# Cross attention with an adapter: queries and output as fp32r products of halves, y and z by DMA, and a new order

## The chip, the cores and the metric

The kernel runs on one core of a Trainium2 chip. The metric is the device time of one execution in microseconds (us); a lower one is better. Times are medians over runs of the same program. The engines are PE (matrix products), DVE (vector), ACT (scalar functions), POOL (general) and SP, which here only issues the DMAs. PE's results go to banks of 512 columns in PSUM; other operands lie in SBUF.

## The reference

Two batches of 2048 rows of 640 features, eight heads of 80 features. Of 128 context tokens 124 are text, and the last four feed an adapter.

```python
query = hidden_states @ Wq
keyt = enc @ Wk
valt = enc @ Wv
hs = _mha(query, keyt, valt)
ca_q1 = jnp.einsum('btc,th->bch', ca, Wq_ca)
ca_q1 = ca_q1[:, indices, :]
ca_hs1 = _mha(ca_q1, residual, residual)
ca_q2 = ca_hs1 @ Wq
ca_hs2 = _mha(ca_q2, ca_k2, ca_v2)
out = hs + ca_hs2
out = out @ Wout + b_out
out = out + residual
```

`indices` spreads 384 rows of `ca_q1` over the 2048 rows; `residual` is x. All inputs and the output are fp32.

## The kernel before

The rows are cut in eight blocks of 512 (four a batch) and in 16 units of 256, two for each block. The work has two strands.

*The text strand.* A block of x is loaded (`xi`) and transposed on DVE (`xt`). `queries_fast` multiplies it by Wq: 640 features are five chunks of 128; the first four form a 2 x 2 scheme in which seven products of halves, with sums of halves of x (`x_sums`) and of Wq (`wq_sums`), stand for eight, and the fifth chunk is multiplied plainly. Block 0 is multiplied plainly altogether (`pq_first`). DVE or ACT take the results out of the bank, DVE adds the second ones (`q<-q,pq`). Parts of the fifth chunk travel through memory to other partitions (`away`, `landing`, then `rests`). For each tile of 128 rows, text scores `sc` follow, their maxima `m` on DVE, exponentials `p` on ACT, a division on POOL (seldom DVE), a transpose `eb` on DVE, a trip through memory (`kept`, `pT`), and the products `ph` with the values, which give `hs`. `text_out_fast` multiplies `hs` by Wout in products `po` of 320 columns, again seven for eight with sums of `hs` and of Wout, and DVE adds each product to the rows of x that will be stored (`x_more`, `last_rows`).

*The adapter strand.* For each block, `yz_block` makes `yz` on PE (`pyz`), ACT copies it out; its y rows are transposed (`yt`) and go through memory, its z rows are taken out by a shuffle on DVE (`zs`), for batch 1 by way of memory (`zb`), and split in two fp32r parts (`zop`). In `adapter`, each batch has 24 score tiles of 128 x 2048, called s1 (row `s<-zop,cop`), of which DVE takes maxima (`mx`). After the last of them the maxima are gathered (`most`, `turned`), go through memory into the operand `cop`, and 24 score tiles of a second kind, s2 (`s<-cop,zop`), are made with it, put through an exponential on ACT (`ea`) and multiplied with y (`acc`). s1 and s2 share a single room of four banks (`quad`): a score tile can be written only when the one before has been read.

*The order.* Nothing is scheduled at run time. The class `Desk` has a table, `ORDER`: a list of task numbers written out; each entry lets the next step of that task be issued, a letter choosing the engine (a ACT, v DVE, g POOL). Every engine works through its own queue in exactly that order. A `Room` counts buffers: a step that needs one stands in the table behind the step that frees it. The helper `matmul` pins each product in place and cuts an fp32 weight of 128 columns into four strips of 32, unless PE is already in the full shape:

```python
wide = rows > 64 and cols > 64 and self.mode != (P, P)
for c in range(0, cols, 32) if wide else (0,):
```

Lines 211, 226 and 236 of the profile are the helpers that issue PE's products, the other engines' instructions and SP's transfers; the groups are told apart by their tiles.

Of the kernel before, what the change touches and what calls it, by code (L numbers as in the profile page):

```python
# [14 lines left out]
P = 128  # L15
HEADS = 8
T = 4
# [28 lines left out]
class Do:  # L46
# [4 lines left out]
    def __init__(self, engine, fn, after=None, needs=(), frees=(), marks=()):  # L51
        self.engines = (engine,) if isinstance(engine, str) else engine
        self.fn, self.after, self.needs, self.frees, self.marks = fn, after, needs, frees, marks
        self.slots, self.value = [], None
# [12 lines left out]
class Desk:  # L67
# [3 lines left out]
    SIDES = {"a": "ACT", "v": "DVE", "g": "POOL"}  # L71
# [3 lines left out]
        2 2 2 2 2 2 36 0 0 0 4 4 0 0 0 0 0 0 0 0 4 0 0 111a 6 6 6 0 4 6 4 2 2 2 2 2 2 2 4 113a 107 108 109 110 4 6  # L75
        114a 115a 3 6 3a 3 116v 4 6 3a 3 3v 6 3 8 8 7 7 7 2 15 15 15 11 15 15 12 8 7 0 0 118a 8 5 15 15 15 15 10 7
        117a 15 7 8 7 7 7 120a 9 1 119v 8 6 121a 7 7 7 7 122a 7 7 124v 9 123v 125a 126a 8 8 127 8 9 8 36 5 128 8 8 8 5
        9 9 9 129 5 130 15 36 15 15 131 9 9 14 14 9 14 14 14 14 9 14 6 112 136a 133a 135v 134v 14g 137 36 112 11 112
        15 14 15 36 14 12 14g 36 138 138 138 36 138 138 12 12 12 36 144v 145v 12 36 36 11a 9 9 9 139 11 9 9 9 140 143a
        9 146a 12 13 101 17 106 140 140 140 140 141 18 6 140 140 140 140 142 106 132 132 16 17 147g 148g 132 101v 142  # L80
        132 101v 101g 101g 101g 39 152 152 152 152 152 152 151 17 17 36 36 156a 142 142 142 18 18 18 18 18 18 18 18
        132 142 16 151 152 36 36 142 16 16 157a 43 151 152g 149g 152 16 132 16 101v 101 18 16 16g 36 159 159 16 36 158
        36 101g 150g 101g 17 160a 159 159 16 151 161a 16g 155 18 18 18 152 162 36 153 36 18 158 158 18 158 155 17 155
        153 36 20 20 19 163 159 159 163 163 21 21 171 163 142 142 158 172 164 163 163 36 21 21 172 172 172 172 21 43
        154 36 154 175 175 165 159 36 175 175 175 175 19 19 19 159g 166g 167g 159 36 36 170 39 181a 36 170 21 21 21 21
        172 172 172 19 20 19 19 182 177 176 177 182 175 19g 19 177 177 159 173 36 20 183a 170 20 36 168g 182 182 182
        182 172 19 184a 20 178 170 178 182 169g 175g 17 21 21 21 21 21 21 22 19g 177 174 177 185 23 182g 36 36 185 185
        186a 185 185 175 24 24 24 24 24 175 24 174 174 24 24 188 24 174 187 185 36 22 47 22 22 22 192 22 180 194 179
        36 180 192 192 192 192 22 192 22g 182 190 174 182 36 179 180 36 195 192 196 36 47 174 174 174 158 20 23 202 23
        23 24 24 24 197 22 197 198g 192g 199v 36 192 36 24 201g 24 206a 197 197 197 22 200g 197 23 202 23 208 51 207a  # L90
        208 174 189 208 208 208 208 197 197g 22g 36 209 209 36 202 205 209 214a 209 192 132 197 189 158 189 189 189
        197 132 189 202 36 215a 209 205 189 209 36 216 55 36 203 205 209 217 217 24 209g 36 26 26 217 217 217 217 209
        217 27 27 27 27 27 158 209 210 27 212 27 204 36 204 203 218 51 36 36 225 224 219g 220g 222g 221g 217g 36 193
# [89 lines left out]
    def run(self):  # L183
        for entry in self.ORDER.split():
# [7 lines left out]
            for room, i in op.frees:  # L192
                room.give(i)
            for k in op.marks:
                self.event(k).known = True
# [44 lines left out]
def kernel(  # L240
# [788 lines left out]
    def queries(n, after, first=False):  # L1029
# [5 lines left out]
        def room(s):  # L1035
            q_of[n] = q_slot(s[0], f"q_{n}"), s[0]
# [1136 lines left out]
```

## Time and profile before

| | |
|---|---|
| median of 3 runs | 564.87 us (564.87 to 565.77) |
| span of the profiled execution | 562.6 us, from its first to its last instruction |
| PE busy | 554.5 us (99%) |
| DVE busy | 386.4 us (69%) |
| ACT busy | 265.7 us (47%) |
| POOL busy | 198.4 us (35%) |

The span is the profiled execution's time from the first to the last instruction; the median of the runs is 2.3 us above it, and what lies around the span has no row of its own. A row of a group reads: line, engine, operation, output <- inputs, partitions x elements, number; then the busy time in us and the mean of one in ns; then the time that the engine sat idle ahead of them and who ended it. A row of the timeline begins with start and duration in us. A row of the stretches gives start and end, the length, and for each engine its busy time and number of instructions, then the granted clock, the share of the DMA engines and GB/s. Products overlap in PE's pipeline, so the distance between starts, not the duration, is what one costs.

### The profile page before, as it was taken

The page shows a single profiled execution, that of the slowest core. Times are in us where ns is not written, and L with a number is a line of the kernel's source. Part 1 is how long each engine was busy: PE and PEld are TensorE (multiplying, and loading weights), DVE is VectorE, ACT ScalarE, POOL GpSimd, SP SyncE. Part 2 cuts the span into 40 slices and gives each one's busy share as a digit, 9 for nine tenths or more (in the row PEclk, how much of TensorE's full clock was granted, in tenths as well). Part 3 has the DMA queues.
Part 4 walks back from the last instruction along what each step waited for, and adds up shares of the span by engine and source line. Part 5 has one row for each costly group of instructions (what it writes and reads, how often), then busy time and mean ns, then how long its engine had stood idle before and what let it go on. Part 6 is the DMA issues. An engine that isn't in the chain of part 4 may idle for free.

```text
span 562.6 us, 18845 instructions
## 1 busy us (share of the span) xinstructions
PE 554.5 (99%) x8088; PEld 314.4 (56%) x8088; DVE 386.4 (69%) x622; ACT 265.7 (47%) x733; POOL 198.4 (35%) x211
## 2 busy tenths in 40 slices
PE   9999999999999999999999999999999999999997
PEld 8563445456555555555465445455545666666664
DVE  1457999999996564579999998655635655555534
ACT  3122645445338898886525424579878230100100
POOL 7002534434524523013559364512330513321310
PEclk9999999999999999999999999999999999999999
DMA  8994769774877889455568895758853687688603
GB/s 264 240 172 127 154 119 161 165 169 141 162 198 163 179 249 172 140 170 172 170 138 248 217 236 133 241 163 255 252 165 108 181 186 192 150 262 229 203 28 142
DMA packets 151699, 101.48 MB, mean 180 GB/s; under 512 B 86492, under 2 KB 130156, under 8 KB 151616
## 3 DMA queue, kind: packets, MB, share of 16 engines
q1 hardware_dynamic: 150848, 99.88, 69.6%
q8 instruction: 64, 1.05, 0.8%
q0 software_dynamic: 768, 0.40, 0.4%
q14 instruction: 19, 0.16, 0.1%
HBM read 61.34 MB, written 38.90 MB: 178 GB/s over the span
## 4 chain that ended last, share of the span: by engine, by line
PE 91%; DVE 3%; DMA 3%; ACT 1%; SPq 1%; POOL 1%; issue 0%; ACTq 0%; DVEq 0%
PE po L211 26%; PE pq L211 25%; PE acc L211 8%; PE sc L211 7%; PE ph L211 7%; PE s L211 7%; PE pq_first L211 3%; PE pyz L211 3%; DVE mx L226 2%; PE pk L211 1%; PE unread L215 1%; DMA zb<-z 1%; DMA x_more<-in_x_dram 1%; DMA first_rests<-away 1%; SPq L236 1%; PE pt_wq L219 1%
## 5 line engine op out<-in xcount | busy, mean ns | idle before, releaser
L226 DVE TENSOR_REDUCE mx<-s 128x4 f32<-128x2048 f32 x48 | 109.2, 2275 | 2.5 <-PE s L211 2.4
L226 ACT ACTIVATE p<-sc,m 128x124 f32<-128x124 f32 x256 | 89.5, 374 | 32.2 <-DVE m L226 32.2
L226 ACT ACTIVATE ea<-s 128x2048 f32<-128x2048 f32 x48 | 90.4, 1884 | 26.5 <-PE s L211 26.2
L226 POOL TENSOR_TENSOR p<-p,r 128x992 f32<-128x992 f32 x28 | 51.9, 1857 | 132.9 <-DVE r L226 126.1
L211 PE MATMUL po<-wout_sums,hs 128*32 128x320 f32 (+1 forms) x1012 | 77.8, 433 | 0.5 <-DVE x_more L226 0.5
L211 PE MATMUL po<-wout_sb,hs 128*32 128x320 f32 (+2 forms) x972 | 77.1, 429 | 0.0
L226 DVE TENSOR_TENSOR x_more<-x_more,po 128x320 f32<-128x320 f32 x72 | 33.7, 480 | 42.6 <-PE po L211 42.6
L226 ACT ACTIVATION_READ_ACCUMULATOR p<-sc,m 128x1 f32 x256 | 55.4, 217 | 0.0
L211 PE MATMUL pq<-xt,wq_sb 128*32 128x256 f32 x896 | 54.3, 381 | 0.5 <-DVE q L226 0.5
L211 PEld LDWEIGHTS po<-wout_sums,hs 128*32 128x32 f32 (+1 forms) x1012 | 37.5, 110 | 29.7 <-issue 1.6
L211 PEld LDWEIGHTS po<-wout_sb,hs 128*32 128x32 f32 (+1 forms) x972 | 36.7, 111 | 27.4 <-issue 0.9
L211 PE MATMUL acc<-ea,y_sb 128*32 128x384 f32 (+2 forms) x768 | 50.4, 384 | 0.0
L226 DVE TENSOR_REDUCE m<-sc 128x4 f32<-128x496 f32 x64 | 40.8, 663 | 13.6 <-PE sc L211 13.4
L226 POOL TENSOR_TENSOR hs<-hs 128x256 f32<-128x256 f32 x35 | 27.5, 790 | 63.5 <-DVE hs L226 54.7
L211 PE MATMUL ph<-pT,vpad 128*32 128x256 f32 x768 | 46.7, 380 | 0.2 <-ACT p L226 0.2
L226 DVE TENSOR_TENSOR last_rows<-last_rows,po 128x320 f32<-128x320 f32 (+1 forms) x57 | 26.4, 473 | 24.8 <-PE po L211 24.7
L226 DVE STREAM_TRANSPOSE eb<-p 128x1024 f32<-128x1024 f32 x32 | 39.5, 1234 | 5.3 <-POOL p L226 3.3
L211 PEld LDWEIGHTS pq<-xt,wq_sb 128*32 128x32 f32 x896 | 27.5, 110 | 22.9 <-issue 5.5
L226 ACT COPY hs<-ph 128x512 f32<-128x512 f32 (+1 forms) x23 | 12.1, 541 | 58.9 <-PE ph L211 58.6
L211 PE MATMUL pq<-xt,wq 128*32 128x512 f32 x320 | 38.8, 595 | 0.0
L211 PEld LDWEIGHTS sc<-kmain,q 64*128 64x128 f32 x512 | 31.8, 187 | 11.9 <-issue 7.5
L211 PE MATMUL sc<-kmain,q 64*128 64x124 f32 x512 | 37.5, 283 | 0.2
(197 smaller groups left out, 792.3 us busy)
## 6 DMA issues: line engine op xcount, KB each, us to landing
kept<-eb SPq DMA_DIRECT2D x32, 512.0 KB
pT<-kept SPq DMA_DIRECT2D x48, 256.0 KB
landing<-away SPq DMA_DIRECT2D x60, 128.0 KB
xi<-in_x_dram SPq DMA_DIRECT2D x28, 256.0 KB
x_more<-in_x_dram SPq DMA_DIRECT2D x18, 320.0 KB
out_dram<-x_more SPq DMA_DIRECT2D x18, 320.0 KB
last_rows<-in_x_dram SPq DMA_DIRECT2D x14, 320.0 KB
y<-yt SPq DMA_DIRECT2D x16, 256.0 KB
```

The costliest lines, as they stand in the source:

```text
L211: self.pin(self.nc.tensor.matmul(out[strip], lhsT[:, strip], rhs, **kw))
L215: self.pin(self.nc.tensor.matmul(out, zeros, zeros, start=True, stop=True))
L219: self.pin(self.nc.tensor.transpose(out, in_, ident))
L226: return lambda *args, **kw: self.pin(getattr(engine, what)(*args, **kw))
L236: self.pin(self.nc.sync.dma_start(out, in_))
```

## The change

Each operand of the query and output products is split into a top half, rounded to fp32r after a factor of 1 - 2^-13, and the rest, low. With a third operand, mix = top - 2^12 low, the fp32 product is put together from three fp32r products: top by top plus low by low (in one bank, `pq` or `po`), and mix by mix (`pm`), added with the factors 1 + 2^-12 and -2^-12. A chunk of 128 query features thus takes 5 + 5 + 5 products of 512 columns, and half of an output tile 5 + 5 + 5 of 320. The seven-for-eight schemes and their sums go. The parts of x (`top`, `low`, `mix`) are made on ACT, DVE and POOL (`part_of`, `mix_of`), those of `hs` in `hidden_parts`, those of the weights in `weight_part`. Block 0's queries stay plain fp32.

z no longer goes through the shuffle: four DMAs write its rows to memory and four for each half bring them back repeated (`z_rows`), in both batches. The fifth chunk's parts come back straight in fp32r. There are two rooms for queries for three, two sets of `hs` parts for three, and three of x (two, and a third when the setup's rows are free), which now also hold a block's top and low. Wout is loaded and split after the last block's queries. And `ORDER` is another table altogether; two of its lines, and the core of the rest:

```diff
...
-        2 2 2 2 2 2 36 0 0 0 4 4 0 0 0 0 0 0 0 0 4 0 0 111a 6 6 6 0 4 6 4 2 2 2 2 2 2 2 4 113a 107 108 109 110 4 6
...
+    0 52 0 0 0 0 0 0 0 0 0 0 0 0 0 0 0 4 4 14 2 2 4 131a 122 2 2 4 132a 123 6 6 6 6 6 2 4 134a 124 2 4 135a 125
...
-    banks, xslots, qslots, rows, staging = Room(4), Room(2), Room(3), Room(0), Room(1)
-    first_rows, rests, landing, halves = Room(4), Room(0), Room(0), [Room(0), Room(0)]
+    banks, xslots, qslots, rows, staging = Room(4), Room(2), Room(2), Room(0), Room(1)
+    first_rows, rests, halves, fifths = Room(4), Room(2), [Room(1), Room(1)], Room(1)
...
-            (((a[0][0], b[0][0], None), [], (0, 0)), ((s2, w[:, 1], None), xs[1] + ws[2], (1, 0)),
-             ((s1, w[:, 0], None), xs[0] + ws[1], (0, 1)), ((None, None, (1, 1)), [], (1, 1))),
-            (((a[0][1], b[1][0], (0, 0)), [], (0, 0)),),
-            (((s4, b[1][1], (0, 1)), ws[4], (0, 1)),),
-            (((s3, w[:, 2], None), xs[2] + ws[3], (1, 1)), ((a[1][1], w[:, 3], (1, 0)), xs[3], (1, 0))),
...
+    def top_of(to, whole):
+        if desk.engine == "ACT":
+            desk.a_activation(to, whole, AF.Identity, scale=UNDER)
+        else:
+            (desk.g_tensor_scalar if desk.engine == "POOL" else desk.v_tensor_scalar)(to, whole, UNDER, None, ALU.mult)
+    def minus(to, x, y):
+        (desk.g_tensor_tensor if desk.engine == "POOL" else desk.v_tensor_tensor)(to, x, y, ALU.subtract)
+    def mixed(to, top, low):
+        desk.v_scalar_tensor_tensor(to, low, -UP, top, ALU.mult, ALU.add)
...
+        for k in ("top", "low"):
+            op = yield Do("NONE", take(k), needs=[(xslots, 1)], marks=[("parts", n)] if k == "low" else [])
+            p[k], room_of[k, n] = op.value
+        for i in range(NCH):
+            yield Fork(part_of(n, i, t, p))
+        yield Do(
+            "NONE", lambda: None, [("low", n, i) for i in range(NCH)] + [("yz read", b, sb)], frees=[(xslots, at)],
+            marks=["last raw"] if n + 1 == len(blocks) else [],
+        )
+        yield Do("NONE", lambda: None, [("x used", n, c) for c in range(NCH)])
+        p["mix"] = p["low"]
...
+        for c in (NCH - 1, *range(NCH - 1)):
+            yield Fork(query_chunk(n, c))
...
+            pq = bank(s[0], f"pq_{n}_{c}")
+            for i in range(NCH):
+                matmul(pq, wq_part("top", i, c), p["top"][:, i], start=(i == 0), stop=False)
+            return pq
...
+                matmul(pq, wq_part("low", i, c), p["low"][:, i], start=False, stop=(i == NCH - 1))
...
+                desk.v_tensor_scalar(to, pq, 1.0 + DOWN, None, ALU.mult)
...
+                matmul(pq, wq_part("mix", i, c), p["mix"][:, i], start=(i == 0), stop=(i == NCH - 1))
...
+            "DVE", lambda: desk.v_scalar_tensor_tensor(to, pq, -DOWN, to, ALU.mult, ALU.add),
...
-                desk.v_stream_shuffle(
-                    zs, yz[:, u, :], [Y + t for t in range(T)] * 4 + [ONE] * 2 + [G - 1] * 14
...
+                dma(away[g], yz[G * g + Y : G * g + Y + T])
...
+                    dma(z_rows[G * g : G * g + MAX], away[g, :, u].unsqueeze(0).to_broadcast([4, T, 512]))
+                return z_rows
...
+    def hidden_parts(m, c0, n, hs, ph, s, at):
+        def cols(k):
+            return hs[k][:, c0 : c0 + n].rearrange("p c t -> p (c t)")
+        src = ph[:, : n * 2 * P]
+        yield Do(EITHER, lambda: top_of(cols("top"), src), [at], marks=[("hs top", m, c0)])
+        yield Do(
+            "DVE", lambda: minus(cols("low"), src, cols("top").bitcast(F32)), frees=[(banks, s)],
+            marks=[("hs low", m, c0)],
+        )
+        yield Do(
+            "DVE", lambda: mixed(cols("mix"), cols("top").bitcast(F32), cols("low").bitcast(F32)),
...
+        steps = [(k, c) for k in kinds for c in range(NCH)]
+        for n, (k, c) in enumerate(steps):
+            matmul(
+                po[:, :HALF], hs[k][:, c, P * i : P * (i + 1)], w_parts["wout", k][:, c, HALF * u : HALF * (u + 1)],
+                start=(n == 0), stop=(n == len(steps) - 1),
+            )
+        return po
...
+            desk.v_scalar_tensor_tensor(t, po[:, :HALF], factor, t, ALU.mult, ALU.add)
...
-            (((a[0][0], w[0][0], None), one_h, ((0, 0),)), ((s2, t2, None), [("hs", m, "s2")], ((1, 0),)),
-             ((s1, t1, None), [("hs", m, "s1")], ((0, 1),)), ((None, None, (1, 1)), end_h, ((1, 1),))),
-            (((s3, t3, None), [("hs", m, "s3")], ((1, 1),)), ((a[1][1], t4, (1, 0)), both_h + end_h, ((1, 0),))),
-            (((a[0][1], w[1][0], (0, 0)), both_h + end_h, ((0, 0),)),),
-            (((s4, w[1][1], (0, 1)), [("hs", m, "s4")] + end_h, ((0, 1),)),),
...
```

Three places show how the new table moves the instructions. The first is DVE between maxima of s1 in batch 0 (the numbers in s1 are batch, block, third, half; those in q, pq and pm a block and a chunk). Before:

```order
L226 TENSOR_REDUCE mx_0_469<-s1_0_1_1_0_1039 128x4
L226 TENSOR_REDUCE m_0_3_0_1084<-sc_0_3_0_1066 128x4
L226 TENSOR_REDUCE m_0_3_1_1085<-sc_0_3_1_1067 128x4
L226 TENSOR_TENSOR q_1_775<-q_1_775,pq_1_1_978 128x2x256
L226 RECIPROCAL r_0_2_882<-r_0_2_882 128x8
L226 TENSOR_REDUCE mx_0_469<-s1_0_1_1_1_1104 128x4
L226 STREAM_TRANSPOSE eb_1_0_1149<-p_1_715 128x1024
L226 TENSOR_REDUCE mx_0_469<-s1_0_1_2_0_1151 128x4
L226 STREAM_SHUFFLE zs_0_2_0_1224<-yz_0_2_1130 128x512
L226 TENSOR_REDUCE m_0_1_0_1193<-sc_0_1_0_1175 128x4
```

After:

```order
L241 TENSOR_REDUCE mx_0_361<-s1_0_1_1_0_1160 128x4
L241 SCALAR_TENSOR_TENSOR q_1_801<-pm_1_3_1175,q_1_801 128x512
L241 STREAM_TRANSPOSE eb_1_1_1184<-p_1_694 128x1024
L241 TENSOR_REDUCE mx_0_361<-s1_0_1_1_1_1187 128x4
L241 SCALAR_TENSOR_TENSOR q_1_801<-pm_1_2_1193,q_1_801 128x512
L241 SCALAR_TENSOR_TENSOR q_1_801<-pm_1_1_1129,q_1_801 128x512
L241 SCALAR_TENSOR_TENSOR q_1_801<-pm_1_0_1168,q_1_801 128x512
L241 STREAM_TRANSPOSE eb_0_1_1204<-p_0_693 128x1024
L241 TENSOR_REDUCE mx_0_361<-s1_0_1_2_0_1208 128x4
```

Between the maxima of tiles 0_1_1_0 and 0_1_2_0 stood two m, an addition and an eb; now four additions of mixed products and two eb stand there, and the shuffles that follow are gone.

The second is PE right behind the last s1 of batch 0, up to the first y/z product of batch 1, while the maxima are gathered for the first s2. Before:

```order
L211 MATMUL s1_0_3_2_1_2034<-zop_0_3_1411,cop_153 128x512 x4
L211 MATMUL pq_4_3_1981<-x_sums_729,wq_sb_98 32x256 x16
L211 MATMUL pq_4_0_1908<-x_sums_729,wq_sums_718 32x256 x16
L211 MATMUL pq_4_3_1981<-xt_1_0_1562,wq_sb_98 32x256 x8
L211 MATMUL pq_4_1_2114<-xt_1_0_1562,wq_sb_98 32x256 x16
L211 MATMUL pq_4_0_1908<-xt_1_0_1562,wq_sb_98 32x256 x8
L211 MATMUL pq_4_1_2114<-xt_1_0_1562,wq_sb_98 32x256 x8
L211 MATMUL pyz_1_0_0_2154<-xt_1_0_1562,wyz_101 32x512 x2
```

After:

```order
L226 MATMUL s1_0_3_2_1_1833<-zop_0_3_1421,cop_157 128x512 x4
L226 MATMUL pm_3_3_1882<-low_3_1530,wq_mix_839 128x512 x5
L226 MATMUL pm_3_0_1889<-low_3_1530,wq_mix_839 128x512 x5
L226 MATMUL pyz_1_0_0_1907<-xt_1_0_1621,wyz_99 32x512 x2
L226 MATMUL pyz_1_0_1_1908<-xt_1_0_1621,wyz_99 32x512 x2
```

Six groups of fp32 products (16 or 8 strip instructions each) stood there; now two groups of five fp32r products do.

The third is DVE between maxima of s1 in batch 1. Before, additions of output products stand between them:

```order
L226 RECIPROCAL r_1_4_3927<-r_1_4_3927 128x8
L226 TENSOR_TENSOR x_more_3630<-x_more_3630,po_7_0_4035 128x320
L226 TENSOR_REDUCE mx_1_3043<-s1_1_2_0_1_4044 128x4
L226 TENSOR_REDUCE m_1_5_1_4032<-sc_1_5_1_4014 128x4
L226 TENSOR_TENSOR x_more_3630<-x_more_3630,po_7_2_4053 128x320
L226 TENSOR_TENSOR x_more_3630<-x_more_3630,po_7_0_4035 128x320
L226 TENSOR_REDUCE mx_1_3043<-s1_1_2_1_0_4077 128x4
L226 TENSOR_TENSOR x_more_3630<-x_more_3630,po_7_0_4035 128x320
L226 STREAM_TRANSPOSE eb_10_0_4122<-p_0_714 128x1024
```

After:

```order
L241 TENSOR_REDUCE m_1_10_1_3633<-sc_1_10_1_3615 128x4
L241 TENSOR_REDUCE mx_1_2544<-s1_1_2_0_0_3698 128x4
L241 STREAM_TRANSPOSE eb_13_1_3746<-p_0_693 128x1024
L241 TENSOR_REDUCE mx_1_2544<-s1_1_2_0_1_3740 128x4
L241 TENSOR_REDUCE m_1_8_0_3768<-sc_1_8_0_3750 128x4
L241 TENSOR_REDUCE m_1_8_1_3769<-sc_1_8_1_3751 128x4
L241 TENSOR_REDUCE mx_1_2544<-s1_1_2_1_0_3773 128x4
L241 RECIPROCAL r_1_8_3770<-r_1_8_3770 128x8
L241 SCALAR_TENSOR_TENSOR q_7_3508<-pm_7_1_3783,q_7_3508 128x512
```

The output additions have left this place; what stands there is text maxima, a transpose and the addition of a query chunk of the last block.

More of the change, by code (lines that the diff above doesn't have):

```diff
@@ L1418, in yz_block @@
[L1418 to L1431 removed]
+        away = hbm.tile([4, T, 2, 512], F32, tag=f"z_{sb}", name=f"z_{b}_{sb}")
@@ L1464, in y_rows @@
         yield Do(
-            "NONE", lambda: None, [("zop", b, sb, u, "away") if b else ("zop", b, sb, u) for u in range(2)] + both,
+            "NONE", lambda: None, [("z out", b, sb)] + both,
             frees=[(yzs, 0)],
```

951 lines of the change are left out of this document (427 added, 524 removed).

## Prediction

> **What bounds the kernel now.** I read the page's engine totals and the clock first, then the chain that ended last, then the busy time by stage, then the rows of the costly groups.
>
> ```profile
> span 562.6 us, 18845 instructions
> PE 554.5 (99%) x8088; PEld 314.4 (56%) x8088; DVE 386.4 (69%) x622; ACT 265.7 (47%) x733; POOL 198.4 (35%) x211
> PEclk9999999999999999999999999999999999999999
> PE 91%; DVE 3%; DMA 3%; ACT 1%; SPq 1%; POOL 1%; issue 0%; ACTq 0%; DVEq 0%
> ```
>
> PE is busy 99%, at full clock, and carries 91% of the chain. The reader should not stop there: DVE's 69% is a mean. So the second view cuts the span at the adapter's maxima (mx, the reduce of a score tile s of 2048 columns). The cuts are the first mx of batch 0, its last, the first of batch 1, its last.
>
> ```profile
> core 0: us, PE busy (x) PEld busy (x) DVE busy (x) ACT busy (x) POOL busy (x), PEclk, DMA share, GB/s
> 0.00:46.00 46.00, 44.87 (x368) 30.47 (x372) 19.43 (x78) 11.96 (x23) 12.98 (x53) 1.00 0.88 218
> 46.00:159.70 113.70, 112.43 (x1684) 59.74 (x1680) 105.02 (x129) 52.63 (x202) 47.70 (x38) 1.00 0.72 156
> 159.70:252.20 92.50, 92.42 (x1435) 50.83 (x1428) 58.03 (x99) 75.49 (x180) 26.12 (x23) 1.00 0.75 177
> 252.20:344.00 91.80, 89.80 (x1275) 46.43 (x1279) 88.19 (x97) 43.20 (x149) 52.00 (x45) 1.00 0.74 196
> 344.00:562.60 218.60, 214.98 (x3346) 126.93 (x3341) 115.78 (x224) 82.40 (x185) 59.63 (x54) 1.00 0.64 180
> L226 DVE TENSOR_REDUCE mx<-s x48: 2239/2282/2294, 46.0 to 344.0; 128x4 f32<-128x2048 f32 x48
> ```
>
> I call the five stages A to E. In B and D, DVE is busy 105.02 of 113.70 us and 88.19 of 91.80 us: it is a second bound right under PE. In C and E it has room. A cheaper PE can be cashed in A, C and E, but in B and D only down to DVE's sum.
>
> **The price of the products.**
>
> ```profile
> L211 PE MATMUL pq<-xt,wq_sb 128*32 128x256 f32 x896 | 54.3, 381 | 0.5 <-DVE q L226 0.5
> L211 PE MATMUL pq<-xt,wq 128*32 128x512 f32 x320 | 38.8, 595 | 0.0
> L211 PE MATMUL s<-zop,cop 32*128 32x512 f32 x4 | 0.5, 490 | 0.0
> L211 PE MATMUL s<-cop,zop 32*128 32x256 f32 x4 | 0.4, 379 | 0.0
> 251.67 0.50 PE L211 MATMUL s<-zop,cop 32*128 32x512 f32 x4
> 252.10 2.78 PE L211 MATMUL pq<-xt,wq 128*32 128x512 f32 x24
> 254.81 0.50 PE L211 MATMUL s<-cop,zop 32*128 32x384 f32 x8
> 255.25 1.07 PE L211 MATMUL acc<-ea,y_sb 128*32 128x128 f32 x16
> 256.25 1.16 PE L211 MATMUL sc<-kmain,q 64*128 64x124 f32 x16
> 257.16 0.64 PE L211 MATMUL sc<-krest,rests 64*128 64x124 f32 x8
> 257.74 0.50 PE L211 MATMUL s<-cop,zop 32*128 32x256 f32 x8
> ```
>
> An fp32 product is recorded twice for each strip of 32 columns; the four strips run side by side. 256 more columns make a record 595 − 381 = 214 ns longer, 0.836 ns per column; two records make 1.67. (The 24 records from 252.10 to 254.81 are three products in 2.71 us.) The fp32r scores s have one record per product, and 256 more columns cost 490 − 379 = 111 ns, 0.434 ns per column. So fp32r is a quarter of fp32 here, if a full 128x128 fp32r product, which no row shows, streams like four 32-row ones side by side. From above, 0.86: the 384 + 128 columns between 254.81 and 255.25 took 0.44 us with loads and the change of tile shape in it. I take 0.434, because it is a difference of two rows and free of both; 0.86 goes to a rival.
>
> Queries of blocks 1 to 7, before: 252 products of 256 columns at 0.428 and 35 of 512 at 0.856, 137.9 us; after, 7 x 5 x 15 = 525 of 512 at 0.222, 116.6. Output before: 288 products of 320 columns at 0.535, 154.1; after, 960 at 0.139, 133.4. Together −42 us. The program changes tile shape about 34 times more; one change costs at most 0.21 (0.43 for a score from 251.67, less its 0.22), so up to +7, and from below 0. PE alone therefore says −35 to −42, a span near 523.
>
> **The stages one by one.** *A.* The order moves the text values (12 products of 320 columns, 6.4 us, and three of 160, 0.8) and three query products of block 0 (2.6) ahead of the first score: 46.0 + 9.8 = 55.8. The new trip of z through memory (out and back) lies beside them; without that cover it would be two trips, each like the 2.1 us from the DMA at 347.48 to that at 349.61 (below).
>
> *B.* PE gets 65 pm and 150 pq products x 0.222 = 47.7, eleven text tiles at 1.49 (256.25 to 257.74) = 16.4, 23 scores at 0.43 = 9.9, three y/z products at 1.7 (four records of 0.43) = 5.1: 79 us. DVE's prices:
>
> ```profile
> L226 DVE TENSOR_REDUCE m<-sc 128x4 f32<-128x496 f32 x64 | 40.8, 663 | 13.6 <-PE sc L211 13.4
> L226 DVE STREAM_TRANSPOSE eb<-p 128x1024 f32<-128x1024 f32 x32 | 39.5, 1234 | 5.3 <-POOL p L226 3.3 <-DMA kept<-eb 2.0
> L226 DVE TENSOR_TENSOR x_more<-x_more,po 128x320 f32<-128x320 f32 x72 | 33.7, 480 | 42.6 <-PE po L211 42.6
> L226 DVE STREAM_TRANSPOSE xt<-xi 128x512 f32<-128x512 f32 x35 | 22.7, 682 | 1.7 <-DMA xi<-in_x_dram 1.7
> L226 DVE TENSOR_TENSOR q<-q,pq 128x512 f32<-128x512 f32 x28 | 18.6, 671 | 4.7 <-PE pq L211 4.6
> L226 DVE STREAM_SHUFFLE zs<-yz 128x512 f32<-128x512 f32 x16 | 11.8, 739 | 0.0
> L226 DVE TENSOR_TENSOR x_sums<-xt 128x512 f32<-128x512 f32 x2 | 2.5, 1243 | 0.0
> L226 DVE TENSOR_TENSOR x_sums<-xt,x_sums 128x512 f32<-128x512 f32 x2 | 1.4, 685 | 0.0
> L226 POOL TENSOR_TENSOR x_sums<-xt 128x512 f32<-128x512 f32 x12 | 15.4, 1282 | 2.7 <-ACT rests L226 2.7
> ```
>
> The 23 maxima stay, 52 us. Out of B go six shuffles (−4.4), two row transposes and two yt (−2.7), the Strassen sums and rests (−4.4); in come one m and one eb (+1.9), three parts of x and one of Wq (+2.8); the query adds stay about even (−0.7). Net −7.5: 97.5 us. PE's 79 lies under it, so B lasts 97.5 plus some idle time, 99.
>
> *C.* PE loses 75 products of 256 and 12 of 512 (−42.4), gains 160 of 512 (+35.5) and a text tile (+1.5), and about 4 of acc and s work goes to D: 92.4 becomes 83. At its start stands the joint from the last maximum to the first score of the second kind, which the other batch shows:
>
> ```profile
> 343.43 0.51 PE L211 MATMUL s<-zop,cop 32*128 32x512 f32 x4
> 343.99 2.29 DVE L226 TENSOR_REDUCE mx<-s 128x4 f32<-128x2048 f32 x1 [0.20 <-PE s L211]
> 347.48 0.31 SPq L236 DMA_DIRECT2D most<-turned  x1
> 349.61 1.16 SPq L236 DMA_DIRECT2D ca<-most  x2
> 352.34 0.94 ACT L226 ACTIVATE cop<-ca,low_c 128x768 fp32r<-128x768 f32 x1 [4.89 <-DMA ca<-most]
> 355.63 0.51 PE L211 MATMUL s<-cop,zop 32*128 32x384 f32 x8
> ```
>
> It is 12.2 us long. In batch 0 PE has 5.9 us of other products left for it after the change (two pm products, a y/z product, a text tile and the score itself), so up to 6 us open; I take 4: C is 87.
>
> *D.* Here the order puts outputs later and conversions earlier. DVE loses sixteen output adds (−7.7), two shuffles (−1.5) and the sums (−3.0); it gains two m and one eb (+2.6), four row transposes of x and a rest (+3.4), two yt (+1.4), three query adds (+2.0), the ph adds that make low halves of hs (+3.5) and seven parts of x (+4.7). Net about +5.4: 88.2 becomes 93.6, with idle time 96, against 91.8 before. D gets longer, though PE's share falls to 79 there (89.8, less 36 output and 56 query products, 46.7, and ten of ph, 4.3; plus 20 and 150 fp32r ones, 36.1, a text tile and some acc, 4).
>
> *E.* PE loses about 252 output products (−134.8), gains 940 (+130.7), ten ph products (+4.3), loses three text tiles (−4.5): 215 becomes 211, and with before's 3.6 of idle time 214. By the same prices DVE gets some 29 us more here, 48 mixed parts of hs foremost, on 115.78 of 218.60; it stays under PE, since each unit's parts are made while PE is on the unit before.
>
> SP issues 511 transfers for 426: 85 x 0.31 = 26 us more in a queue of its own, spread over the span; I cost that at nothing, as z's small transfers are wanted only when the next quarter of scores begins.
>
> Sum: 55.8 + 99 + 87 + 96 + 214 = 551.8 against the span of 562.6. The median of the runs, 564.87, is 2.3 above the profiled span, so 554 us.
>
> Two-source DVE work on SBUF is slower beside POOL: x_sums<-xt took 1243 beside it and x_sums<-xt,x_sums 685. The change raises such work from 7 to 24 instructions in C and 43 to 60 in E, but in B and D, which DVE bounds, only from 7 to 9, so at 0.56 each and POOL busy half the time it adds 1 us there. The Trainium skill ("SBUF — State Buffer", Who interferes with whom) has a rule that speaks against the change: a DVE instruction with two SBUF inputs and a GpSimd one that reads SBUF exclude each other for the whole instruction. By it each of the 34 new ones in C and E could cost a whole POOL instruction, 17 x 1.28 = 22 us of DVE in either: C's DVE, about 58 + 10 by the prices, would come to 90 and C with it, 557 us in all against 554. The trace's 0.56 bears out the direction and not the full size.
>
> **Rivals.**
>
> *PE's saving arrives whole.* If the maxima wait less than I think, because C and E take up what DVE leaves, the time is 523 + 2.3, about 525. For it: PE's 99% before. Against: DVE's 105.02 and 88.19 in B and D, whose maxima nothing removes.
>
> *Slower: the parts of x form a chain with three buffers.* A block's raw rows, top and low fill all three x slots, so the next block's tops wait for the last pm product of this one. One block takes 0.6 + 5 x 1.28 on POOL for the lows, 25 x 0.222 of PE, 7.0 again for the mixed ones and 5.6 of PE: 25 us with every engine at hand, while B offers 99 / 2.6 = 38 us per block (13 of the 35 query chunks end there). POOL's p and ACT's exponentials stand between. If waiting stretches the chain past 39.5 us, seven blocks lose the gain of 11; at 41.5 the time is 554 + 7 x 3.5 = 578.
>
> *fp32r on the full array costs 0.86 per column.* Then 525 x 0.44 + 960 x 0.275 = 495 for 292 before: some 765 us.
>
> *The clock falls.* PE will idle in B and D, 17 to 20 us each over 23 scores, 0.8 at a time in the mean. If the clock halved through both, PE's 79 would become 158 in each, for 99 and 96, and the time 675. The trace never shows idle PE, only a clock of 1.00. The Trainium skill ("TensorE: Matmul & The Clock Gate", Part 1) states that an idle window of about 3.4 us halves the clock; pauses of 0.8 would not do it, a single long one would, for a few us.
>
> **How the numbers follow.** Forecast 0.58 (545 to 566), PE's saving whole 0.14, the chain 0.20, dear fp32r 0.03, clock 0.05. The likeliest gives 554. To leave out no more than 2 in 10, the range runs from 527, beside the PE case, to 580, past the chain. A change within 0.2% (563.7 to 566.0) can't be told from none: 0.05. Faster 0.69: the PE case and most of the forecast. Slower 0.26.
>
> **What would show it.** Right: DVE busy over 95% between the maxima of each batch while PE drops to 80% there; stage D longer than 91.8; pm and pq products 0.22 apart; E near 214 with PE still at 98%. Wrong: PE waiting on low or mix from POOL (the chain), a clock under 1.00 in B or D, or stages B and D at PE's sum (79 in each).

## The result, and the profile after

The changed kernel takes 668.67 us (median of 4 runs, 661.25 to 670.67) against 565.32 for the kernel before on the same chip: ratio 1.180, interval 1.173 to 1.186. It is slower by 103 us; the forecast was 554 and its range ended at 580. The page of the changed kernel, totals, clock and chain:

```profile
span 666.1 us, 13121 instructions
...
PE 577.9 (87%) x5069; PEld 411.6 (62%) x5069; DVE 449.2 (67%) x675; ACT 285.9 (43%) x769; POOL 255.8 (38%) x234
...
PEclk9998866989889999999995967989999799899999
...
PE 48%; DMA 18%; DVE 13%; issue 7%; SPq 6%; ACT 4%; POOL 3%; POOLq 0%; DVEq 0%; ACTq 0%
```

Before, PE held 91% of the chain. Now it holds 48%, and no other engine has taken the rest: transfers, DVE, the queues and ACT share it. PE's busy time did not fall but rose by 23 us, though fewer product instructions run (5069 for 8088), and its clock is no longer full. The same five stages, cut at the same maxima (columns as before):

```profile
0.00:59.32 59.32, 54.61 (x548) 34.01 (x548) 28.74 (x91) 17.08 (x39) 24.29 (x62) 1.00 0.81 197
59.32:192.35 133.03, 108.87 (x623) 73.41 (x615) 98.40 (x101) 60.42 (x222) 68.55 (x52) 0.82 0.60 137
192.35:289.78 97.43, 91.37 (x904) 58.18 (x904) 76.27 (x108) 78.98 (x203) 37.77 (x30) 1.00 0.64 139
289.78:411.73 121.95, 93.48 (x703) 59.69 (x704) 98.18 (x100) 56.07 (x185) 82.73 (x61) 0.85 0.55 148
411.73:666.10 254.37, 229.54 (x2302) 186.29 (x2300) 147.65 (x280) 73.31 (x122) 42.44 (x31) 0.97 0.55 150
...
L241 DVE TENSOR_REDUCE mx<-s x48: 2239/2279/2294, 59.3 to 411.7; 128x4 f32<-128x2048 f32 x48
```

| stage | before | forecast | after | over the forecast |
|---|---|---|---|---|
| A | 46.0 | 55.8 | 59.3 | 3.5 |
| B | 113.7 | 99 | 133.0 | 34 |
| C | 92.5 | 87 | 97.4 | 10 |
| D | 91.8 | 96 | 122.0 | 26 |
| E | 218.6 | 214 | 254.4 | 40 |

In B and D, DVE's sums came out close to what was worked out (98.40 for 97.5, 98.18 for 93.6), but DVE is busy for only 74% and 81% of these stages, and PE for 82% and 77%. Both engines wait. What PE itself waited for, over the whole span (us in total, times, longest), after and then the longest such rows of before:

```profile
PE ph L226 <- DMA pT<-p: 21.7, 4, 8.6
PE s L226 <- DVE mx L241: 19.0, 14, 2.8
PE pm L226 <- POOL low L241: 5.2, 2, 4.0
PE ph L226 <- DMA pT<-kept: 3.6, 1, 3.6
```

```profile
PE unread L215 <- DVE zeros L226: 1.1, 1, 1.1
PE s L211 <- DVE mx L226: 1.1, 2, 0.8
```

Before, PE hardly waited for anything. After, two things stand out: the products `ph` that wait for pT to come back from memory, and waits that go round through other engines. In B the longest rows of all engines were these:

```profile
ACT low L241 <- PE pq L226: 20.3, 4, 6.8
POOL zop L241 <- ACT zop L241: 18.5, 5, 8.2
POOL low L241 <- ACT low L241: 18.1, 5, 7.1
ACT zop L241 <- DMA z_rows<-z: 17.2, 5, 6.2
ACT p L241 <- DVE m L241: 17.1, 6, 8.2
PEld pm L226 <- POOL low L241: 11.5, 6, 4.3
```

Read it as a ring: ACT's scaling of a low part (in place, for the mixed operand) waits for PE's last product that reads it, POOL's subtraction for ACT, PE's product `pm` for POOL. Each link is in an in-order queue, with z's parts and the softmax behind it. In E the timeline of PE and of SP shows the other wait:

```profile
507.72 1.05 PE L226 MATMUL ph<-pT,vpad 128*32 128x256 f32 x16
...
508.83 1.73 SPq L251 DMA_DIRECT2D pT<-kept  x4
510.60 0.31 SPq L251 DMA_DIRECT2D pT<-p  x1
...
517.40 1.93 PE L226 MATMUL ph<-pT,vpad 128*32 128x256 f32 x16 [8.64 <-DMA pT<-p]
```

The transfers that refill a pT room start at 508.83, as soon as the ph from 507.72 has emptied it, and the next entry of PE's table is a ph that needs them: 8.64 us of nothing. pT lives in the query rooms, of which the change leaves two for three.

The clock, in windows of 3.41 us (PE's busy time, granted clock, DMA share, GB/s), around one fall and the rise after it:

```profile
349.35:352.76 3.41, 1.82 (x28) 1.00 0.85 234
352.76:356.17 3.41, 0.78 (x4) 0.50 0.53 118
356.17:359.59 3.42, 2.88 (x20) 0.50 0.00 0
359.59:363.00 3.41, 3.41 (x32) 0.50 0.66 121
363.00:366.41 3.41, 3.41 (x11) 0.50 0.69 207
366.41:369.83 3.42, 2.84 (x14) 1.00 0.75 188
```

A window in which PE was busy 1.82 of 3.41 us was enough to halve the clock, and it came back only behind full windows, though not behind every one: the window from 359.59 was full, and the next one still ran at half clock. There are twelve such stretches, 102 us together.

### The profile page after: what moved, and what is told of

It reads as the page before. It is cut to its first block, busy times and chain, and to the rows that moved or that the text cites. A ratio compares the mean times of both kernels' runs of the same rounds, so it can differ in the third digit from the quotient of the medians.

```text
span 666.1 us, 13121 instructions
## 1 busy us (share of the span) xinstructions
PE 577.9 (87%) x5069; PEld 411.6 (62%) x5069; DVE 449.2 (67%) x675; ACT 285.9 (43%) x769; POOL 255.8 (38%) x234
## 4 chain that ended last, share of the span: by engine, by line
PE 48%; DMA 18%; DVE 13%; issue 7%; SPq 6%; ACT 4%; POOL 3%; POOLq 0%; DVEq 0%; ACTq 0%
PE po L226 8%; PE pq L226 8%; PE pm L226 8%; SPq L251 6%; PE acc L226 5%; PE ph L226 5%; DVE mx L241 4%; PE sc L226 4%; DMA pT<-p 4%; PE s L226 4%; DMA out_dram<-rows 3%; DMA pT<-kept 3%; ACT p L241 2%; DMA out_dram<-row 2%; PE pyz L226 2%
## 5 line engine op out<-in xcount | busy, mean ns | idle before, releaser
L226 PE MATMUL po<-wout_top,hs 128*128 128x320 f32 x320 | 61.6, 324 | 3.5 <-DVE rows L241 2.1
L226 PE MATMUL pm<-low,wq_mix 128*128 128x512 f32 x175 | 54.9, 456 | 9.2 <-POOL low L241 5.2
L226 PE MATMUL po<-wout_low,hs 128*128 128x320 f32 x320 | 58.1, 312 | 0.0
L226 PEld LDWEIGHTS po<-wout_top,hs 128*128 128x128 f32 x320 | 50.1, 193 | 12.6 <-DVE rows L241 3.4
L226 PE MATMUL pm<-wout_mix,hs_mix 128*128 128x320 f32 x320 | 53.0, 311 | 1.0 <-DVE row L241 1.0
L226 PE MATMUL acc<-ea,y 128*32 128x384 f32 (+2 forms) x768 | 51.2, 392 | 0.2 <-ACT ea L241 0.2
L226 PE MATMUL pq<-top,wq_top 128*128 128x512 f32 x175 | 49.5, 419 | 1.6 <-ACT p L241 1.2
L226 PEld LDWEIGHTS pm<-low,wq_mix 128*128 128x128 f32 x175 | 35.4, 216 | 24.4 <-POOL low L241 12.2
L226 PEld LDWEIGHTS po<-wout_low,hs 128*128 128x128 f32 x320 | 50.5, 191 | 0.0
L226 PE MATMUL pq<-low,wq_low 128*128 128x512 f32 x175 | 49.5, 422 | 0.8 <-DVE low L241 0.8
```

Of the source, the lines that this page charges most:

```text
L226: self.pin(self.nc.tensor.matmul(out[strip], lhsT[:, strip], rhs, **kw))
```

## The experiments

Each is an edit of the changed kernel unless it says otherwise; "ratio" is to the kernel before on the same chip, with its 95% interval. The stages are spans of the profiled execution, the clock its mean.

| run | us | ratio | clock | A, B, C, D, E |
|---|---|---|---|---|
| the change | 668.67 | 1.180 [1.173, 1.186] | 0.92 | 59, 133, 97, 122, 254 |
| half_before | 564.29 | 0.998 [0.995, 1.001] | 1.00 | 46, 114, 93, 91, 218 |
| half_after | 661.79 | 1.167 [1.155, 1.180] | 0.90 | 59, 134, 96, 121, 253 |
| no_mix | 646.81 | 1.143 [1.135, 1.150] | 0.93 | 60, 116, 97, 118, 254 |
| top_only | 644.97 | 1.136 [1.129, 1.143] | 0.92 | 59, 120, 92, 119, 254 |
| no_mix_half | 638.32 | 1.127 [1.122, 1.132] | 0.94 | 59, 113, 96, 114, 255 |
| parts_dve | 685.53 | 1.211 [1.198, 1.224] | 0.90 | 60, 144, 99, 129, 254 |
| z_shuffle | 666.89 | 1.178 [1.170, 1.186] | 0.93 | 59, 131, 98, 122, 255 |
| no_pm_out | 657.96 | 1.162 [1.144, 1.181] | 0.89 | 60, 135, 98, 121, 238 |
| rows_pool | 678.55 | 1.203 [1.194, 1.212] | 0.91 | 60, 133, 97, 121, 267 |
| pt_once | 635.09 | 1.123 [1.119, 1.127] | 0.94 | 59, 134, 98, 113, 231 |
| pt3 | 648.49 | 1.146 [1.142, 1.151] | 0.93 | 59, 134, 98, 121, 236 |
| no_mix_pt_once | 617.13 | 1.088 [1.081, 1.094] | 0.95 | 59, 120, 97, 108, 231 |
| fill4 | 676.39 | 1.193 [1.178, 1.209] | 0.94 | 59, 135, 98, 128, 251 |
| fill8 | 691.11 | 1.219 [1.207, 1.232] | 0.96 | 59, 146, 99, 133, 249 |
| fillgap | 671.41 | 1.190 [1.182, 1.198] | 0.95 | 59, 138, 98, 122, 252 |
| replan | 698.34 | 1.236 [1.230, 1.242] | 0.90 | 67, 130, 115, 127, 256 |

**Is DVE the bound of B and D?** half_after and half_before take the maxima over half of each bank:

```diff
-lambda q4=op.value: desk.v_tensor_reduce(mx[:, ct, u, :, sb], q4, AX.X, ALU.max),
+lambda q4=op.value: desk.v_tensor_reduce(mx[:, ct, u, :, sb], q4[:, :, :256], AX.X, ALU.max),
```

> The changed kernel with each of the 48 maxima over 256 of the 512 columns of each of its four rows of scores, so that half of them is left out; 48 x 1.1 = 53 us less of DVE work in stages B and D. Theory DVE BOUND (the prediction's): B and D follow DVE, and the time falls by 35 to 50 us. Rival CHAIN: B and D wait for the parts of x and for transfers as well, DVE was busy only 74% and 81% of them, and the time falls by less than 20.

> The kernel before with each of the 48 maxima over half of the columns, 53 us less of DVE work. If PE bounds the kernel before (98% busy in B and D), the time falls by less than 5 us; if DVE bounds B and D as well, by 10 to 40.

B and D of half_after:

```profile
58.82:192.40 133.58, 110.80 (x623) 75.09 (x615) 75.01 (x101) 60.90 (x226) 68.52 (x52) 0.80 0.60 136
288.88:409.74 120.86, 97.91 (x701) 63.22 (x702) 73.31 (x100) 56.10 (x185) 81.58 (x61) 0.79 0.54 145
```

DVE has 23 and 25 us less to do, and the stages last as long as they did. DVE does not bound B or D. The kernel before does not react either: there PE binds.

**The chain of the parts of x.** no_mix leaves the mixed operand of x unmade; the products `pm` read the low part:

```diff
-            if desk.engine == "ACT":
-                desk.a_activation(t, t.bitcast(F32), AF.Identity, scale=UP)
-            else:
-                mixed(t, top.bitcast(F32), t.bitcast(F32))
+            pass
...
-            lambda: both and minus(t, top.bitcast(F32), t.bitcast(F32)), marks=[("mix", n, i)],
+            lambda: None, marks=[("mix", n, i)],
```

> The changed kernel without the making of the mixed operand of x (24 scalings on ACT with 24 subtractions on POOL, 11 combined steps on DVE); the products pm read the low part as it is, so PE has the same work. The DVE bound is out (half the maxima changed 7 us). Theory CHAIN: block by block, top, low, products, mix, products run one behind the other through three buffers, and B and D wait for them; with half of the links gone the time falls by 20 to 45 us, B from 133 to below 120. Rival ORDER: the waits come from elsewhere in the queues (z, text, transfers), and the time falls by less than 10.

```profile
59.64:175.82 116.18, 101.26 (x631) 68.59 (x615) 97.81 (x100) 52.79 (x208) 51.61 (x38) 0.87 0.67 155
```

B loses 17 us and D 4.5. DVE's work in B is unchanged (97.81 for 98.40): what went are ACT's and POOL's links between two products of PE, 8 and 17 us of work on engines that were busy for about half of the stage. So these links carried 17 us that no engine's sum shows. Not all of it is waiting: PE's pauses in B fall from 24 to 15 us, and its busy time falls by 8, with a clock of 0.87 for 0.82.

top_only also leaves the low parts out (all products read the top part), and no_mix_half adds the halved maxima to no_mix:

```diff
...
-            ADDS, lambda: minus(as_rows(p["low"][:, i]), t[:, :, i], as_rows(p["top"][:, i].bitcast(F32))),
+            ADDS, lambda: None,
...
```

> On top of no_mix the low parts of x aren't made either: all three products of a query chunk read the top part, so that no subtraction on POOL and no scaling on ACT stands in front of them; only the tops are made. Theory 1 (the chain of the parts is what stretches B and D past DVE's and PE's sums): B falls from 116 in no_mix to about DVE's own sum there, 95 to 102, D from 117 to 100 to 108; 615 to 630 in all. Theory 2 (the rest of B and D is z's and the softmax's links): within 6 us of no_mix's 647.

> no_mix with the maxima mx over a quarter... half of each bank (256 of 512 columns), which takes about 23 us of DVE out of B and of D. If DVE's sum becomes the bound once the mixed parts are gone, B falls from 116 to about 100 and the time to 620 to 632; if the in-order chain still holds, it stays within 7 us of no_mix's 647.

Neither gives what its first theory asked for: 645 and 638 us after no_mix's 647. Taking 23 us more out of DVE in B gives 3 there, 3.5 in D. The subtractions for low show no cost in B and D beyond the mixed parts' links, but they do in C (no_mix, then top_only):

```profile
175.82:272.98 97.16, 92.30 (x904) 58.27 (x904) 69.22 (x101) 77.92 (x201) 34.76 (x28) 0.98 0.65 142
178.97:271.26 92.29, 90.01 (x900) 57.75 (x900) 58.29 (x94) 76.18 (x193) 24.66 (x21) 0.98 0.67 147
```

C is 5 us shorter without them; as B is 4 us longer, at a clock of 0.83 for 0.87, the total does not show it. What holds B at 113 to 120 is neither the low parts nor DVE's sum. PE is busy 101 us of no_mix's 116, for 79 by the prices at full clock. A clock of 0.87 means some 30 us of this stage at half clock, so half clock explains at most 15 of the 22 us; the rest stays open.

parts_dve gives POOL's subtractions of x's parts to DVE, to take one queue out of the ring:

```diff
+            if self.engine == "POOL" and op.fn.__qualname__.split(".")[-3] in ("part_of", "mix_of"):
+                self.engine = "DVE"
```

> The changed kernel with the 49 subtractions that make low and mixed parts of x moved from POOL (1.28 us each) to DVE (about 0.67), at the same places of the order; nothing is left out. Theory CHAIN: POOL's slow links become shorter, the time falls by 15 to 40 us although DVE gets 33 us more. Rival DVE BOUND: slower by 10 to 35. Rival ORDER: within 10.

It costs 17 us, 11 of them in B and 7 in D. That is the number of the rival that calls DVE the bound, but DVE is not: it is busy 112 of 144 us in B. POOL's other entries now wait longer, for ACT and for DVE. B as a whole, and POOL's two longest rows in it (18.5 and 13.9 in the changed kernel):

```profile
60.23:204.19 143.96, 109.81 (x613) 75.95 (x611) 112.29 (x125) 60.60 (x222) 35.88 (x26) 0.78 0.53 123
...
POOL zop L243 <- ACT zop L243: 45.0, 7, 16.3
POOL p L243 <- DVE r L243: 40.1, 8, 15.8
```

We read it so: an instruction that moves to another in-order queue puts its wait in front of everything behind it there. The run does not separate that from DVE's 14 us of added work in B.

**z.** z_shuffle brings back the shuffle on DVE in batch 0:

```diff
...
+                if not b:
+                    desk.v_stream_shuffle(
+                        z_rows, yz[:, u, :], [Y + t for t in range(T)] * 4 + [ONE] * 2 + [G - 1] * 14
+                    )
```

> The changed kernel with batch 0's z rows taken out by the shuffle on DVE, as in the kernel before (8 x 0.74 us), and not by way of memory; batch 1 stays. If the trip through memory holds up the scores of stage B (the chain shows z coming back there four times, 2.4 to 3.5 us each), the time falls by 5 to 15 us; if it is hidden, within 4.

The interval covers that of the change; B is 2 us shorter. z's trip, though it stands in B's waits with 17.2 us, carries next to nothing as long as the other waits stand beside it.

**What holds E?** no_pm_out leaves the 320 mixed output products and their additions out; rows_pool has POOL issue the loads of the residual rows:

```diff
...
-            "PE", lambda s: out_product(m, i, u, hs, s, ("mix",), "pm"),
+            "PE", lambda s: None,
```

```diff
-                dma(t, x[b, st * P : (st + 1) * P, :])
+                desk.g_dma_start(t, x[b, st * P : (st + 1) * P, :])
```

> The changed kernel without the 320 mixed products of the output (47 us of PE at 0.147) and their 64 additions on DVE. If PE bounds stage E, E falls from 254 by 40 to 47 us. If the transfers of the probabilities and the waits for them bound it (PE stood for 25 us in E), it falls by less than 30.

> The changed kernel with the loads of x's rows for the output issued by POOL and not by SP. In the changed kernel SP's queue stood 68 us behind such loads, which wait until the store that used the buffer has landed, with the loads of the probabilities queued behind them. Theory SP QUEUE: E loses 10 to 25 us of 254. Rival PE: E was busy 229.5 of 254.4 on PE, so it loses less than 8.

E of no_pm_out:

```profile
413.95:652.22 238.27, 194.18 (x1982) 145.20 (x1980) 122.20 (x216) 73.03 (x122) 43.18 (x32) 0.90 0.60 160
```

PE has 35 us less to do there and E shrinks by 16; PE's idle time grows from 25 to 44 us. The clock is lower, too (0.90 for 0.97), which is why products worth 47 us at 0.147 take only 35 off. E isn't bound by PE alone. rows_pool made E 12 us longer: POOL's own entries then waited for stores for their buffers (57.9 us, the row below), and SP's waits moved to other rows. So this edit moved the wait into a queue that has other work behind it; whether SP's row loads hold E, it does not settle.

```profile
POOL rows L241 <- DMA out_dram<-rows: 57.9, 7, 15.7
```

pt_once leaves the transfers back into pT out for units 2 to 15, and pt3 keeps them all but adds a third room, made of buffers that are free by then:

```diff
...
-                lambda: dma(
+                lambda: m < 2 and dma(
...
```

```diff
...
+    third = const.tile([P, 4, 512], F32, name="third")
+    half_tiles = [third[:, i].rearrange("p (a n) -> p a n", a=2).bitcast(F32R) for i in range(2)]
+    q_fifth = third[:, 2]
+    z_rows = third[:, 3]
...
+            pTs.give(2)
...
```

> Each of the two pT rooms is loaded once; for units 2 to 15 the five transfers back into pT are left out, so the text outputs of those units are made from the first two units' probabilities and the second attention's rows of batch 0. Products, parts, stores and the rest are unchanged. Theory 1 (in E, PE waits for the reload of a pT room, of which the change leaves two for three, and SP's queue stands still meanwhile): E falls from 254 by the 25 us of PE idle in it and its half clock, to 222 to 232, D by the 11 us of its last gaps; 625 to 640 in all. Theory 2 (E is held by its output rows, loads and stores, and the trips of pT only take the blame because they come last): E within 8 us, 655 to 668.

> A third pT room in the changed kernel, made of buffers whose work is over by then (both halves, the fifth chunk and z's rows, put in one tile), given once the last of them has been used; every product, part, transfer and entry of the table is kept, so PE still asks for each ph where it did, but the reload of a room waits for the ph three units back, not two. If the two rooms are the cause of what pt_once took away, E falls from 254 to between 231 (pt_once) and 240, and D by a few us: 640 to 652. If it is the trip itself, whichever room it goes to (SP's queue or the 1 MB per unit), the time stays within 8 us of the changed kernel, 660 to 672.

E of pt_once, then of pt3, and pt3's longest row of PE waiting for pT over the whole span (both times lie in D):

```profile
404.29:635.01 230.72, 222.35 (x2301) 182.67 (x2300) 150.51 (x280) 73.22 (x122) 46.52 (x35) 1.00 0.35 111
```

```profile
411.65:648.11 236.46, 226.51 (x2302) 184.91 (x2300) 150.05 (x280) 73.34 (x122) 43.29 (x32) 0.99 0.61 162
...
PE ph L226 <- DMA pT<-p: 11.6, 2, 8.2
```

Without the reload E falls by 24 us, PE is busy 96% of it and the clock is full. A third room brings 18 of the 24 with every transfer in place. The cut from three rooms to two is the largest cause found in E: half of the 36 us by which this stage is longer than before. pt3 still does all the work; it is 20 us better than the change and 83 worse than the kernel before. The third room serves from the fourth load of a room on, at 437.8 us: D, in which the first three lie, gains 1 us from it and 8.5 from pt_once.

no_mix_pt_once joins the two edits:

> The edit of no_mix (the mixed operand of x isn't made) and that of pt_once together. If the two waits lie in different stages (B and D the one, E and D the other) the gains add: 668 - 22 - 33, some 610 to 620. If both only uncover the same next wait, the sum is much less than that, above 630.

617.13 us: 51.5 below the change, where the two alone give 21.9 and 33.6. They nearly add, so they are separate costs. Against the kernel before, the stages then stand at +13, +6, +5, +16 and +12 us.

**The clock.** fill4 and fill8 put 4 or 8 small products with the identity matrix into a free bank ahead of a score tile s1; fillgap puts them into 21 of the pauses over 0.6 us that the trace of the change shows (fill4's edit is the one below):

```diff
+                        if banks.free and banks.free[0] < 4 and (sb or ct or u):
+                            spare = bank(banks.free[0], f"spare_{b}_{sb}_{ct}_{u}")
+                            for _ in range(4):
+                                desk.warm(spare[:, :P], ident)
```

> The changed kernel with four products of the identity with itself (fp32, 128 columns, 0.21 us each at full clock) ahead of every first-kind score tile at which a bank is free, 31 of 48; their results go into that spare bank and are not read. It adds up to 27 us of PE work and takes nothing away. Theory CLOCK: the changed kernel's PE pauses at those scores, its clock is halved after such pauses (12 times, 101 us in all), and a share of the loss comes from that. Then the clock rises to 0.96 or more and the time falls by 15 to 45 us, to 625 to 655. Rival QUEUES: the time is set by DVE, POOL and transfers in stages B and D and the low clock only fills PE's slack; then the clock rises as well, but the time stays at 660 to 672, or rises by up to 27.

> As with four, but eight products at each of these places, up to 53 us of added PE work. Theory CLOCK: clock 0.97 or more; the time is below the changed kernel's 668 as long as the filling is shorter than the pauses (about 70 us in all), 620 to 660. Rival QUEUES: 665 to 720, more than with four.

> The changed kernel with products of the identity put only into those 21 pauses of PE over 0.6 us that its trace showed, each a little shorter than its pause (in all 35 us at full clock, two scores without a free bank left out); nothing is taken away. With filling ahead of scores everywhere (27 and 53 us) the clock rose to 0.94 and 0.96 and the time rose by 8 and 22. Theory CLOCK: the fillers lie in time that PE idled, so the time falls with the clock's recovery: on the chain that ended last PE worked 56 us in the half-clock stretches, half of which, 28 us, is the loss; with a clock of 0.97 the time is 640 to 655. Rival: the pauses move and the low clock only filled slack: 662 to 680.

The mean clock rose to 0.94, 0.96 and 0.95, and the time did not fall (fillgap's interval overlaps that of the change). The fillers are work of their own in the same queue: in B of fill8 PE is busy 17 us more at a clock of 0.92 for 0.82, and B is 13 us longer. So these runs don't isolate what the clock costs. An estimate from above: the chain that ended last has some 56 us of PE in the twelve stretches, so at most half of that, 28 us, would be saved at full clock.

**The order.** replan keeps every step on its engine and replaces the table by one from a simple list scheduler that reckons a trip through memory at 3.5 us and starts whatever can start first.

> The changed kernel with another ORDER: the same 2457 steps on the same engines, put in a new sequence by a list scheduler that reckons every trip through memory at 3.5 us behind its transfer and every DVE instruction at its measured length, and then takes the step that can start first. No product, part, transfer or buffer is added or removed. Theory 1 (the sequence is at fault: its queues stand behind trips that come back later than the table allows for): B, D and E shorten, E most, since a product ph no longer stands right behind the reload of its only free pT room; 610 to 640 us. Theory 2 (the work itself sets the time: the parts, their engines, the two pT rooms and the transfers, so that any sequence waits as much elsewhere): within 10 us of the changed kernel, 655 to 680. Theory 3 (the clock is what costs): the time follows the granted clock; with more waiting spread out the clock stays near 0.92 and the time near 660.

698 us. All three theories missed: A, C and D lost 8, 18 and 5 us, B won 3, E stayed at 256. This other order is no better. Whether a good order for these steps exists is not shown either way.

## Why the prediction was wrong

**The failing step** is "B lasts 97.5 plus some idle time, 99", and with it "with idle time 96" for D. It took the sum of the busiest engine for the length of a stage and allowed 2% for waiting. That held in the kernel before because PE was full: every other engine's wait lay beside PE's work. The change took PE's sum in B from 112 to 79 by the prices at full clock, which removed the cover, and what came up was not DVE's sum but waits between the engines, among them the chain from product to part to product. Halving the maxima shows it (23 us off DVE, nothing off B), and so does no_mix (nothing off DVE, 17 off B). That chain is half of the 34 us by which B exceeds the forecast; of D's 26 it is 4.5, and the pT reload 8.5.

The 79 was too low as well: PE is busy 108.9 us in B, and a clock of 0.82 means that some 48 us of the stage ran at half clock, so at full clock at least 85 us would be left (an estimate). And waiting was priced by its mean: "0.8 at a time". The trace has few and long pauses of PE: in B ten of over 0.6 us hold 22 of its 24 us, the longest 4.0, and in D the longest is 8.0.

One sign that was named for being right came true, "stage D longer than 91.8", but by luck: it was to come from a DVE busy over 95%, and DVE is busy 81% of D.

**E under PE, 214.** Forecast 211 of work and 3.6 of idle time; measured 229.5 and 25. The largest part of it is the pT reload: with a third room E is 18 us shorter (15 of idle time, 3 of work), without the reload 24 (16.5 and 7). The change's text named "two rooms for queries for three", and the prediction followed queries and never asked who else lives in these rooms. Of the 18 us of extra work, 7 go with the reload (222.35 in pt_once, at full clock). Most of the rest is the price of a product: in the chain that ended last (start, length, number of products) ten `po` in a row last 1.67 us, twenty 3.13, ten `pq` 2.51, five `pm` of queries 1.34:

```profile
471.21 3.13 PE po L226 x20
...
475.79 1.67 PE po L226 x10
...
209.35 2.51 PE pq L226 x10
...
240.41 1.34 PE pm L226 x5
```

(3.13 − 1.67) / 10 = 0.146 us per product of 320 columns against 0.139, and (2.51 − 1.34) / 5 = 0.234 for 512 against 0.222. For 960 output products that is 7 us. **The price rule was right** to within 6%: an fp32r product of 128 x 128 takes 0.234 us for 512 columns against 0.856 in fp32, about a quarter, and "dear fp32r" is out.

**C, 87, came out at 97.4.** PE is busy 91.4 us there for 83 worked out. The price makes 2 us of it (some 160 products at 0.012 more). The forecast bounded the changes of tile shape at 7 us for the whole program and entered none in the sum; whether they make the other 6 was not tried. What top_only shows is that 5 us of C go with the subtractions for low.

Some of these run on DVE, and here the prediction misread a row. The "1243 beside it" is the mean of two instructions: 1849 ns beside a POOL instruction, with which it overlaps for 1.3 us, and 637 ns alone. One clash thus cost 1.2 us, about as long as the POOL instruction still ran, and not 0.56. In the changed kernel `low<-xt,top` on DVE takes between 0.63 and 2.22 us. Such excess adds up to some 8 us of DVE in C (an estimate from the trace, each instruction against its group without the clash), where DVE is busy 76.3 us for the forecast's 68. The sum had nothing for it. Whether it is what lengthens C was not tried.

**The rivals.** The slower one, "the parts of x form a chain", named the right place and gave 578. Its price was built on one block's 25 us, "with every engine at hand". That condition failed: the links stand in queues with z's parts and the softmax, and no_mix puts the worth of the mixed parts' links at 22 us. "The clock falls" was turned down because a mean pause of 0.8 us could not do it. It did fall, twelve times. That the rival's 675 lies near the measured 668.67 is luck: it had the clock halved throughout B and D, where it was 0.82 and 0.85, and the estimate above leaves the clock 28 us at most. The Trainium skill ("TensorE: Matmul & The Clock Gate", Part 1) asks for an idle window of about 3.4 us; the window's length agrees with the trace (3.41 us), the idleness does not, as shown below.

**SP's queue at nothing.** There are 85 more transfers. z_shuffle, which leaves out 48 for z in batch 0, found no harm in those. But SP's in-order queue stood 41.1 us behind ph to refill pT, 20.5 with the third room, and 30.1 in the kernel before (in this order):

```profile
SPq L251 <- PE ph L226: 41.1, 7, 10.2
```

```profile
SPq L251 <- PE ph L226: 20.5, 5, 6.7
```

```profile
SPq L236 <- PE ph L211: 30.1, 8, 7.2
```

Standing there is no cost by itself: before, PE was busy beside it.

**What stays open:** without the two causes found, the chain of the mixed parts and the pT reload, the kernel is 51.5 us faster, while the stages together exceed the forecast by 114. Not explained are the clock's own share (28 us at most by the estimate above); what keeps B and D 6 and 16 us above the kernel before in no_mix_pt_once, with neither DVE's sum nor the mixed parts; A's 3.5 us, which are not z's trip, since z_shuffle has the same 59 us; and whether another order would do better.

## What to carry to other kernels

An engine's sum bounds a stage from below and no more. When a change empties the engine that was full, follow one piece of work through all the queues it crosses and ask what covers each hop now, because the old cover was that engine's work. And when buffers go from three to two, list every tile that lives in them, not only the one that the change speaks of.

## What the chip showed beside that

The halving of PE's clock doesn't need an idle window. In the changed kernel all 24 falls and rises lie on one grid of 3.413 us. The falls followed windows of 3.41 us with a busy share of 0.00 to 0.59; no window above that was followed by a fall, and the lowest share that was spared is 0.47. The other runs give the same picture, with a wider overlap: the highest share before a fall is 0.64 (rows_pool, the window from 345.58, 2.18 of 3.41 us), the lowest that was spared 0.44 (z_shuffle, from 460.12, 1.49 of 3.41). All twelve rises of the changed kernel came behind a window that was busy throughout, but three other such windows at half clock brought no rise. So a kernel whose PE is about half busy in such a window can pay for its waits a second time; how much that cost here was not isolated.
